# An involution's input turned by VectorE and stored in 128 byte pieces, and a shorter lag for GpSimd while keys are made

## The chip, the cores and the metric

The kernel runs on one core of a Trainium2 chip. The metric is the time of the device in microseconds (us); lower is better. Names used below: PE is TensorE, DVE is VectorE, ACT is ScalarE, POOL is GpSimd, SP is the engine that issues most DMA transfers. Each engine works through its own instructions in order and waits for others through semaphores.

## The reference, cut to what matters

Two layers run one after the other on x, 4 images of 512 channels and 64x64 pixels, all in float32.

```python
# layer 0: attention over the 4096 pixels of each image, CI = 128
q, k, v = wq@x + bq, wk@x + bk, wv@x + bv        # 128 x 4096 each
attn = softmax(q.T @ k, axis=-1)                 # 4096 x 4096
x = wo @ (v @ attn.T) + bo + x
# layer 1: involution with a 7x7 window
o1 = relu(W1@x * s1 + b1)                        # 512 -> 128 channels
w = Ws @ relu(Wr@o1 * sr + br) + bs              # 49 weights per pixel for each of 8 groups of 16 channels
y[c] = sum over 49 taps of w[group(c), tap] * o1[c] shifted by the tap
x = W3@y * s3 + b3 + x
```

## The kernel before, in words

**Attention.** For each image b, `keys_values` goes through eight chunks of 512 pixels (order 2 to 7, then 1, 0), loads x and makes k (matmuls `pk`) and v (`pv`). Then `attention` goes through eight blocks of 512 queries. A block has 32 steps; a step makes one tile of scores (`pss`), ACT takes its exponential into `pt` (five buffers), PE adds `pt` times v into `po`, and DVE adds `pt` into `pacc` (L627), for the softmax's sum. Scores run two steps ahead. A step takes PE 1.72 us when nothing else stands in it.

**What is woven in.** After each step, and several times in each chunk of keys, `chores` advances three generators. `finish_block` ends the block of queries before: it normalizes `on`, runs four matmuls `pwo` (each followed by a DVE add, L513), makes `p1` and `o1`, adds a last bias on ACT (L531), and turns o1 to one pixel per partition: four PE transposes into `pp` (L543), an ACT copy to `o1t` (L546), two transfers into the padded image `pix` in DRAM (L550). Then it makes `pr` and `red`, from which the tap weights come. Its steps are `yield`s; the last image (`late`) uses waits on the planner's clock instead. `involution` works on units of 4 image rows: matmuls `pw` give the tap weights, DVE multiplies them with windows of pixels in `ring` (L339, buffers `prod`, four of them), POOL adds the products to `acc` (L363). `turn_unit` and `close_chunk` turn the sum back (`pa`), run four matmuls `py`, each followed by a DVE add (L417), and store the chunk to `out_dram` (L426).

**The ring.** `pump` loads rows of `pix` into `ring` (L245), 12 rows of windows, as soon as the rows are written and their places are free. It waits on SP for the transfers that wrote them.

**What sets the order.** A planner in Python holds a clock for PE (`pe`) and the times at which DVE, POOL and the DMA will be free by its own costs, and decides at each call whether the next tap product is issued now. The rule that matters here is in `involution`: a product waits while POOL is planned to be more than 7.5 us behind PE. The build then sets each engine's final order, which can move instructions and transfers on a queue by some places; loads of x stand earlier there than the program has them.

**PSUM.** Small matmul results (`pl`, `pwo`, `p1`, `pp`, `pr`, `pa`, `py`, `pq`, and the `spread` that DVE writes) share the tag `mm` with two banks: a result can be written when the one before the last has been read.

Of the kernel before, what the change touches and what calls it, by code (L numbers as in the profile page):

```python
# [8 lines left out]
F32 = mybir.dt.float32  # L9
# [4 lines left out]
B, C, H, W = 4, 512, 64, 64  # L14
N = H * W
P = 128
CT = C // P
CH = 512
NCH = N // CH
RW = CH // W  # L20
# [4 lines left out]
PAD = 3  # L25
# [42 lines left out]
DVE_OP, POOL_OP = 0.7, 1.28  # L68
DVE_TAPS, POOL_TAPS = (0.16, 0.27), (0.19, 0.55)
ROW_US, X_US, PIX_US, LAND_US = 2.2, 3.8, 1.5, 3.0  # L70
HOP_US = 0.8
STEP_US = 1.0
PIECE = 3
TB = 32
WARM = 8
# [5 lines left out]
def fast_path(  # L81
# [20 lines left out]
    nc = tc.nc  # L102

    def pool(name, bufs, **kw):
# [7 lines left out]
    work1 = pool("work1", 1)  # L112
# [3 lines left out]
    ps = pool("ps", 2, space=bass.MemoryType.PSUM)  # L116
# [11 lines left out]
    ident = const.tile([P, P], F32, name="ident")  # L128
# [6 lines left out]
    pix = [  # L135
        scratch.tile([H + 2 * PAD, WP, P], F32, tag=f"pix{i}", name=f"pix{i}") for i in range(2)
    ]
# [9 lines left out]
    pe = 0.0  # L147
    due, seen = 0.0, 0.0
    free = {"dve": 0.0, "pool": 0.0, "dma": 0.0}
    tail = []  # L150
    reds, sums_c = {}, {}
    written = {}
    landing = {}
    low, load = 0, 0

    def until(us):
        while pe < us and not tail:
            yield "wait"

    def pe_us(us):  # L160
        nonlocal pe
        pe += us

    def takes(engine, us):
        free[engine] = max(free[engine], pe) + us
        return free[engine]
# [33 lines left out]
    def w_slice(off, t):  # L200
        return wt[:, off + t * P : off + (t + 1) * P]
# [87 lines left out]
    def involution():  # L289
        nonlocal low, due  # L290
        while True:
            while not units:
                yield "none"
            b, u = units.pop(0)
# [12 lines left out]
            for o, (x, dy, n) in enumerate(ops):  # L307
                if o and dy >= DYS[1][0] > ops[o - 1][1]:
                    low = base + UR
                    pump()  # L310
                    if tail and units:
                        early[units[0]] = weights(*units[0])
                rows = [(base + dy + t * 2) % RING for t in range(NT)]
                while base + dy + n + NT > load:
                    yield "wait"
                landed = max(landing[base + dy + i] for i in range(n + NT))
                while not tail and (
                    pe < max(begin, landed)
                    or free["dve"] > pe + (4.5 if b == B - 1 else 3.5)
                    or free["pool"] > pe + 7.5  # L320
                ):
                    yield "wait"
                free["pool"] = max(free["pool"], takes("dve", DVE_TAPS[0] + DVE_TAPS[1] * n))
                takes("pool", POOL_TAPS[0] + POOL_TAPS[1] * n)
                due -= n
                d0 = dy - DYS[dy >= DYS[1][0]][0]
                first = x == 0 and dy < DYS[1][0]
                prod, p0 = acc, d0
                if not first:
                    prod, p0 = prods.tile(  # L330
                        [P, NT, 4, P], F32, tag="prod", name=f"prod_{b}_{u}_{o}"
                    ), 0
                col = (x * K + dy) * G
                lines = ring[:, rows[0] : rows[0] + n, x, :]
                image = bass.AP(
                    tensor=lines.tensor, offset=lines.offset,
                    ap=[lines.ap[0], [(rows[1] - rows[0]) * K * P, NT], [K * P, n], [1, P]],
                )
                nc.vector.tensor_tensor(  # L339
                    prod[:, :, p0 : p0 + n, :].rearrange("p t d (g c) -> p t d g c", g=G),  # L340
                    image.rearrange("p t d (g c) -> p t d g c", g=G),
                    pw[:, :, col : col + n * G].unsqueeze(3)
                    .broadcast_to([P, NT, n * G, GC])
                    .rearrange("p t (d g) c -> p t d g c", d=n),
                    ALU.mult,
                )
                if first:
                    pass
                elif tail and o % 2 and (accp is not None or n > 1):

                    begin_sum = accp is None
                    if begin_sum:
                        accp = ps1.tile(
                            [P, NT, 2, P], F32, tag=("po", "acc")[u % 2], name=f"accp_{b}_{u}"
                        )
                    for d in range(0, n, 2):
                        k = min(2, n - d)
                        mm(
                            accp[:, :, :k, :], ident, prod[:, :, d : d + k, :],
                            begin_sum and d == 0, o + 2 >= len(ops) and d + 2 >= n,  # L360
                        )
                else:
                    nc.gpsimd.tensor_tensor(  # L363
                        acc[:, :, d0 : d0 + n, :], acc[:, :, d0 : d0 + n, :], prod[:, :, :n, :],
                        ALU.add,
                    )
                yield
# [61 lines left out]
    def keys_values(b):  # L429
        kt = kvpool.tile([P, N], F32, tag="k", name=f"k_{b}")  # L430
        vT = kvpool.tile([P, N // P, P], F32, tag="v", name=f"v_{b}")

        for i, c in enumerate(KEYS):
            for k in KEYS[i + 1 : i + 3]:
                if (b, k) not in xs:
                    load_x(b, k)
            if b < 2 and i == 4:
                for rows in (slice(0, PAD), slice(PAD + H, None)):
                    nc.sync.dma_start(pix[b][rows].rearrange("r w c -> w r c"), zero)
                for cols in (slice(0, PAD), slice(PAD + W, None)):  # L440
                    nc.sync.dma_start(pix[b][PAD : PAD + H, cols, :], zero[:H])
            xt = xs[b, c] if c < KEEP else xs.pop((b, c))
            pk = ps_s.tile([P, CH], F32, tag="s", name=f"pk_{b}_{c}")
            for t in range(CT):
                mm(pk, w_slice(O_WK, t), xt[:, t, :], t == 0, t == CT - 1)
                if t % 2:
                    chores()
            nc.scalar.activation(
                kt[:, c * CH : (c + 1) * CH], pk, AF.Identity, bias=v1(V_BK)
            )  # L450
            pv = ps1.tile([P, 4, P], F32, tag=("po", "acc")[i % 2], name=f"pv_{b}_{c}")
            for j in range(4):
                for t in range(CT):
                    mm(
                        pv[:, j, :], xt[:, t, j * P : (j + 1) * P], w_slice(O_WV, t),
                        t == 0, t == CT - 1,
                    )
                if j % 2:
                    chores()
            nc.scalar.copy(vT[:, 4 * c : 4 * c + 4, :], pv)  # L460
        return kt, vT
# [11 lines left out]
    def finish_block(b, c, off, n, po, sums):  # L473

        late = b == B - 1
        name = f"{b}_{c}_{off}"
# [11 lines left out]
        blocks = work2.tile([P, CH // TB], F32, tag="blocks", name=f"blocks_{name}")  # L488
# [8 lines left out]
        row = (b * N + c * CH + off) // TB  # L497
# [27 lines left out]
        o1 = work1.tile([P, CH], F32, tag="o1", name=f"o1_{name}")[:, :n]  # L525
        nc.scalar.activation(o1, p1, AF.Relu, bias=v1(V_B1), scale=v1(V_S1))

        def last_bias():

            for t in range(CT):  # L530
                nc.scalar.activation(xt[:, t, :], xt[:, t, :], AF.Identity, bias=v1(V_B3 + t))  # L531
                if t % 2:
                    yield

        if late:
            yield from until(pe + HOP_US)
        else:
            yield from last_bias()

        tiles = n // P  # L540
        pp = ps.tile([P, CH // P, P], F32, tag="mm", name=f"pp_{name}")[:, :tiles]
        for t in range(tiles):
            nc.tensor.transpose(pp[:, t, :], o1[:, t * P : (t + 1) * P], ident)  # L543
        pe_us(0.5)
        o1t = work1.tile([P, CH // P, P], F32, tag="o1t", name=f"o1t_{name}")[:, :tiles]
        nc.scalar.copy(o1t, pp)  # L546
        top = c * RW + off // W
        for h in range(2):
            row = PAD + top + h
            nc.sync.dma_start(  # L550
                pix[b % 2][row : row + 2 * tiles - 1 : 2, PAD : PAD + W, :]
                .rearrange("r w c -> w r c"),
                o1t[h * W : (h + 1) * W],
            )
        us = takes("dma", PIX_US) + LAND_US

        pr = ps.tile([P, CH // NT], F32, tag="mm", name=f"pr_{name}")[:, : n // NT]
# [77 lines left out]

    taps = [involution()]
    for b in range(B):
        kv = keys_values(b)
        if b == 0:

            pb = ps.tile([P, CT], F32, tag="mm", name="pb")
            for t in range(CT):
                tc.keep_in_program_order(mm(pb[:, t : t + 1], w_slice(O_WO, t), v1(V_BVC)))
            bo = const.tile([P, CT], F32, name="bo")
            nc.vector.tensor_tensor(bo, pb, vec[:, V_BO : V_BO + CT], ALU.add)
        attention(b, *kv)
# [407 lines left out]
```

## Time and profile before

| | us |
|---|---|
| median of 3 runs | 2645.77 (2645.48 to 2646.93) |
| the profiled execution's own time | 2645.35 |
| its span, first to last instruction | 2643.6 |
| PE busy | 2614.5 |
| DVE busy | 1851.5 |
| POOL busy | 1821.4 |
| ACT busy | 870.0 |

The mean granted clock of TensorE is 0.996. The keys of the four images begin near 5, 620, 1265 and 1910 us; attention of the last image ends near 2560 us, and what follows is the end of the last involution. The 62 transfers of 128 KB into `pix` land 2.5 us after their issue in the median, the loads of x (1 MB) 5.5 us, the stores (1 MB) 4.2 us, and the ring's loads of six rows 15.8 us. In a list of instructions a line gives start, duration, engine, line of the code, operation, output and inputs, shape and count; in square brackets stands the idle time before it and what ended it.

### The profile page before, as it was taken

To read this page: it belongs to the slowest core of one execution; us is meant where nothing else is said; L and a number is where in the kernel's file an instruction comes from. 1 tells how busy PE (TensorE), PEld (TensorE's weight loads), DVE (VectorE), ACT (ScalarE), POOL (GpSimd) and SP (SyncE) were. 2 spreads that over 40 slices of the span, in tenths; PEclk is the share of its full clock that TensorE was granted. 3 is DMA by queue.
4 is the path that set the end of the run, shared out by engine and by line. 5 is a ranking of instruction groups with operands and counts; after the bars stand their busy time and mean duration, and the time that the engine had idled before them with its cause. 6 is when DMAs were issued, how large, how long until landed. Compare 5 with 4: busy or idle time off the path is not lost.

```text
span 2643.6 us, 24069 instructions
## 1 busy us (share of the span) xinstructions
PE 2614.5 (99%) x7478; PEld 1254.9 (47%) x7478; DVE 1851.5 (70%) x2602; ACT 870.0 (33%) x1454; POOL 1821.4 (69%) x1197
## 2 busy tenths in 40 slices
PE   9999999999999999999999999999999999999998
PEld 7444444445544444444554444444464444444574
DVE  0437788776575778778566677878847667787887
ACT  1333333332333333333223333333323333333330
POOL 0007788788761788888784377878888467777875
PEclk9999999999999999999999999999999999999999
DMA  6032323325614233332450423333353423222343
GB/s 233 0 74 60 92 66 77 77 57 140 157 35 105 60 92 92 92 82 65 121 143 13 106 60 92 92 92 92 92 142 107 97 60 85 69 62 61 75 90 100
DMA packets 104730, 231.70 MB, mean 88 GB/s; under 512 B 5576, under 2 KB 24464, under 8 KB 104464
## 3 DMA queue, kind: packets, MB, share of 16 engines
q1 hardware_dynamic: 104160, 229.70, 35.2%
q8 instruction: 61, 1.00, 0.2%
q14 instruction: 77, 0.63, 0.1%
q10 hardware_dynamic: 432, 0.36, 0.0%
HBM read 187.28 MB, written 42.77 MB: 87 GB/s over the span
## 4 chain that ended last, share of the span: by engine, by line
PE 91%; POOL 4%; DMA 2%; DVE 2%; issue 1%; ACT 0%; SPq 0%; POOLq 0%; DVEq 0%; ACTq 0%
PE pss L208 32%; PE po L208 32%; POOL acc L363 4%; PE pq L208 4%; PE p L208 4%; PE py L208 4%; PE pwo L208 4%; PE pv L208 3%; PE pk L208 3%; DMA ring<-pix 2%; PE pw L208 2%; DVE prod L339 1%; PE pr L208 1%; PE pp L543 1%; PE accp L208 0%
## 5 line engine op out<-in xcount | busy, mean ns | idle before, releaser
L363 POOL TENSOR_TENSOR acc<-acc,prod 128x768 f32<-128x768 f32 (+3 forms) x1063 | 1699.6, 1619 | 797.5 <-DVE prod L339 694.7
L208 PE MATMUL pss<-q,k 128*128 128x512 f32 (+1 forms) x2112 | 1055.2, 584 | 2.3 <-ACT q L469 2.3
L208 PE MATMUL po<-pt,v 128*128 128x512 f32 (+1 forms) x2112 | 1047.0, 580 | 0.0
L596 ACT ACTIVATE pt<-pss 128x512 f32<-128x512 f32 x1024 | 611.2, 597 | 1219.0 <-PE pss L208 1198.7
L339 DVE TENSOR_TENSOR prod<-ring,pw 128x512 f32<-128x512 f32 (+3 forms) x1092 | 899.9, 849 | 147.6 <-POOL acc L363 93.4
L627 DVE TENSOR_TENSOR pacc<-pacc,pt 128x512 f32<-128x512 f32 x958 | 665.3, 695 | 415.6 <-ACT pt L596 405.9
L208 PEld LDWEIGHTS po<-pt,v 128*128 128x128 f32 x2112 | 398.6, 190 | 477.5 <-issue 458.7
L208 PEld LDWEIGHTS pss<-q,k 128*128 128x128 f32 x2112 | 389.3, 190 | 455.0 <-issue 436.3
L208 PE MATMUL py<-accT,wt 128*128 128x512 f32 (+1 forms) x264 | 133.0, 587 | 13.8 <-DVE x L513 12.7
L417 DVE SCALAR_TENSOR_TENSOR x<-py,vec,x 128x512 f32<-128x512 f32 (+1 forms) x132 | 96.4, 730 | 53.6 <-PE py L208 51.6
L208 PEld LDWEIGHTS pv<-wt,x 128*128 128x128 f32 x1024 | 123.3, 198 | 14.8 <-issue 14.8
L208 PE MATMUL pwo<-on,wt 128*128 128x512 f32 (+1 forms) x264 | 129.2, 582 | 0.0
L374 POOL TENSOR_TENSOR acc<-acc 128x512 f32<-128x512 f32 x120 | 119.7, 997 | 9.4
L208 PE MATMUL pv<-wt,x 128*128 128x128 f32 x1024 | 126.0, 282 | 0.0
L339 DVE TENSOR_TENSOR acc<-ring,pw 128x1024 f32<-128x1024 f32 (+1 forms) x84 | 79.4, 964 | 62.4 <-PE pw L208 60.6
L531 ACT ACTIVATE x<-x,vec 128x512 f32<-128x512 f32 (+1 forms) x132 | 92.9, 706 | 81.5 <-PE p L208 76.3
L208 PE MATMUL p<-x,wt 128*128 128x512 f32 (+1 forms) x264 | 119.2, 579 | 0.0
L208 PE MATMUL pk<-x,wt 128*128 128x512 f32 x256 | 117.3, 597 | 0.0
L208 PE MATMUL pq<-x,wt 128*128 128x512 f32 (+1 forms) x264 | 115.6, 580 | 0.0
L513 DVE SCALAR_TENSOR_TENSOR x<-pwo,bo,x 128x512 f32<-128x512 f32 (+1 forms) x132 | 96.4, 733 | 23.6 <-PE pwo L208 20.4
L208 PEld LDWEIGHTS py<-accT,wt 128*128 128x128 f32 x264 | 49.5, 191 | 72.9 <-issue 43.3
L208 PEld LDWEIGHTS pq<-x,wt 128*128 128x128 f32 x264 | 49.7, 190 | 58.8 <-issue 52.7
(57 smaller groups left out, 747.7 us busy)
## 6 DMA issues: line engine op xcount, KB each, us to landing
x<-x_dram SPq DMA_DIRECT2D x55, 1024.0 KB, 5.5
ring<-pix SPq DMA_DIRECT2D x74, 448.0 KB, 10.4
ring<-pix SPq DMA_DIRECT2D x24, 1344.0 KB, 15.8
out_dram<-x SPq DMA_DIRECT2D x31, 1024.0 KB, 4.2
ring<-pix SPq DMA_DIRECT2D x24, 896.0 KB, 13.6
ring<-pix SPq DMA_DIRECT2D x30, 672.0 KB, 10.9
ring<-pix SPq DMA_DIRECT2D x6, 2240.0 KB, 21.0
pix<-o1t SPq DMA_DIRECT2D x62, 128.0 KB, 2.5
```

The lines of the kernel that those rows point to most:

```text
L208: return nc.tensor.matmul(o, lhsT=lhsT, rhs=rhs, start=start, stop=stop)
L339: nc.vector.tensor_tensor(prod[:, :, p0 : p0 + n, :].rearrange("p t d (g c) -> p t d g c", g=G), image.rearrange("p t d (g c) -> p t d g c ...
L363: nc.gpsimd.tensor_tensor(acc[:, :, d0 : d0 + n, :], acc[:, :, d0 : d0 + n, :], prod[:, :, :n, :], ALU.add,)
L374: nc.gpsimd.tensor_tensor(acc[:, :, :n, :], acc[:, :, :n, :], acc[:, :, n : 2 * n, :], ALU.add)
L417: nc.vector.scalar_tensor_tensor(xt[:, t, :], py, v1(V_S3 + t), xt[:, t, :], ALU.mult, ALU.add)
L513: nc.vector.scalar_tensor_tensor(xt[:, t, :], pw, bo[:, t : t + 1], xt[:, t, :], ALU.add, ALU.add)
L531: nc.scalar.activation(xt[:, t, :], xt[:, t, :], AF.Identity, bias=v1(V_B3 + t))
L543: nc.tensor.transpose(pp[:, t, :], o1[:, t * P : (t + 1) * P], ident)
L596: nc.scalar.activation(pt, pss, AF.Exp)
L627: nc.vector.tensor_tensor(paccs[k], paccs[k], pt, ALU.add)
```

## The change

First, the lag. The limit of 7.5 us becomes a variable: 4.0 us while `keys_values(b)` runs, 7.5 us in attention.

Second, for images 0 to 2 the turn of o1 changes. DVE transposes the 128x512 tile in blocks of 32x32 into `o1t`, directly after o1. Partition 32i+a then holds, for each run of 32 pixels, pixel a of the run and the 32 channels of group i. PE's four transposes and ACT's copy are gone. Eight transfers, one for each group of channels and half of the image's width, put it in place, each in 256 pieces of 32 floats (128 bytes); before, there were two transfers of 256 pieces of 512 bytes. They are issued three yields after the last bias, and `pr`, `red` and the entry of the units follow them. The last image keeps PE's transposes.

```diff
+POOL_LAG = 4.0, 7.5
@@ involution
-                    or free["pool"] > pe + 7.5
+                    or free["pool"] > pe + lag
@@ finish_block
+        o1t = work1.tile([P, CH // P, P], F32, tag="o1t", name=f"o1t_{name}")[:, :tiles]
         if late:
             yield from until(pe + HOP_US)
+            (transposes pp, copy to o1t and two transfers, as before)
         else:
+            blocks = o1t.rearrange("p t c -> p (t c)")
+            takes("dve", DVE_OP)
+            nc.vector.transpose(
+                blocks.rearrange("p (k q) -> p k q", q=TB), o1.rearrange("p (k q) -> p k q", q=TB)
+            )
             yield from last_bias()
-        (transposes pp, copy to o1t and two transfers, for every image)
+            for _ in range(3):
+                yield
+            for i in range(P // TB):
+                channels = slice(i * TB, (i + 1) * TB)
+                for h in range(W // TB):
+                    columns = slice(PAD + h * TB, PAD + (h + 1) * TB)
+                    nc.sync.dma_start(
+                        pix[b % 2][PAD + top : PAD + top + RW, columns, channels]
+                        .rearrange("r a c -> a r c"),
+                        blocks[channels].rearrange("p (r h c) -> p r h c", r=RW, c=TB)[:, :, h, :],
+                    )
@@ the loop over images
+        lag = POOL_LAG[0]
         kv = keys_values(b)
+        lag = POOL_LAG[1]
```

More of the change, by code (lines that the diff above doesn't have):

```diff
@@ L153, in fast_path @@
     landing = {}
+    lag = 0.0
     low, load = 0, 0
@@ L533, in last_bias @@
                     yield
+        tiles = n // P
+        top = c * RW + off // W
+        o1t = work1.tile([P, CH // P, P], F32, tag="o1t", name=f"o1t_{name}")[:, :tiles]
         if late:
             yield from until(pe + HOP_US)
-        else:
-            yield from last_bias()
[L540 to L554, printed above, removed]
+            pp = ps.tile([P, CH // P, P], F32, tag="mm", name=f"pp_{name}")[:, :tiles]
@@ new lines, in finish_block @@
+            for t in range(tiles):
+                nc.tensor.transpose(pp[:, t, :], o1[:, t * P : (t + 1) * P], ident)
+            pe_us(0.5)
+            nc.scalar.copy(o1t, pp)
+            for h in range(2):
+                row = PAD + top + h
+                nc.sync.dma_start(
+                    pix[b % 2][row : row + 2 * tiles - 1 : 2, PAD : PAD + W, :]
+                    .rearrange("r w c -> w r c"),
+                    o1t[h * W : (h + 1) * W],
+                )
+        else:
+            blocks = o1t.rearrange("p t c -> p (t c)")
[3 more added lines that the diff above has]
+            )
+            yield from last_bias()
+            for _ in range(3):
[4 more added lines that the diff above has]
+                    columns = slice(PAD + h * TB, PAD + (h + 1) * TB)
+                    nc.sync.dma_start(
+                        pix[b % 2][PAD + top : PAD + top + RW, columns, channels]
+                        .rearrange("r a c -> a r c"),
+                        blocks[channels].rearrange("p (r h c) -> p r h c", r=RW, c=TB)[:, :, h, :],
+                    )
```

## The prediction

> **What bounds the kernel now.** I read the busy times first, then what TensorE waits for, then the timeline around its longest wait.
>
> ```profile
> PE 2614.5 (99%) x7478; PEld 1254.9 (47%) x7478; DVE 1851.5 (70%) x2602; ACT 870.0 (33%) x1454; POOL 1821.4 (69%) x1197
> ```
>
> TensorE (PE) is busy for 2614.5 of 2643.6 us. Only two things shorten the program: fewer PE instructions, or fewer of the 29.1 us in which PE stands idle. The waits of PE say where those are:
>
> ```profile
> PE py L208 <- DVE x L513: 12.7, 3, 4.5
> PE accp L208 <- DVE prod L339: 2.4, 1, 2.4
> PE pss L208 <- ACT q L469: 2.3, 3, 0.8
> ```
>
> The first line is three waits, at 650, 1295 and 1940 us: once in each keys stage that has an involution beside it. About 12 us more lie after 2540 us, in the end game. The timeline of PE, then of VectorE (DVE), at the first wait (start, duration, line, names):
>
> ```profile
> 646.97 3.60 PE L208 MATMUL pk<-x,wt 128*128 128x512 f32 x8
> 654.52 1.30 PE L208 MATMUL py<-accT,wt 128*128 128x512 f32 x2 [3.95 <-DVE x L513]
> 655.61 5.24 PE L208 MATMUL pv<-wt,x 128*128 128x128 f32 x32
> 660.69 1.88 PE L208 MATMUL p<-x,wt 128*128 128x512 f32 x4
> ...
> 689.35 3.60 PE L208 MATMUL pk<-x,wt 128*128 128x512 f32 x8
> 692.78 3.73 PE L208 MATMUL pv<-wt,x 128*128 128x128 f32 x32
> 696.36 3.60 PE L208 MATMUL pq<-x,wt 128*128 128x512 f32 x8
> ```
>
> ```profile
> 650.97 0.95 DVE L339 TENSOR_TENSOR prod<-ring,pw 128x768 f32<-128x768 f32 x1 [1.47 <-POOL acc L363]
> 652.85 0.95 DVE L339 TENSOR_TENSOR prod<-ring,pw 128x768 f32<-128x768 f32 x1 [0.93 <-POOL acc L363]
> 653.72 0.75 DVE L513 SCALAR_TENSOR_TENSOR x<-pwo,bo,x 128x512 f32<-128x512 f32 x1
> ```
>
> py needs a `mm` bank of PSUM that the L513 add of the last pwo must read first. That add stands in DVE's order behind five tap products, and each of these waits for GpSimd (POOL) to give back one of four prod buffers. PE falls idle 3.95 us and then runs slowly: pv x32 takes 5.08 us (655.61 to 660.69), against 3.58 at 692.78. From the start of pk to the start of p the undisturbed cost is 3.43 (pk, 689.35 to 692.78) + 0.86 (one py) + 3.58 (pv) = 7.87 us; the trace has 13.72 here, 14.78 (1291.36 to 1306.14) and 13.97 (1936.57 to 1950.54). **The three waits cost 5.9 + 6.9 + 6.1 = 18.9 us**, not 12.7.
>
> **What the Trainium skill says.** "TensorE: Matmul & The Clock Gate", Part 1 (the HAM clock gate): an idle window of about 3.4 us drops the array to half clock until it has been busy again. The trace agrees: granted clock 0.65 from 656 to 660 us, 1.00 from 660. "VectorE: DVE Perf Modes", The three transpose paths: VectorE turns 32x32 blocks only, so a run of contiguous channels after it is 32 floats; no SBUF to SBUF turn is in this trace, and the nearest row is the 718 ns stream transpose of L502. "DMA: Bandwidth & Descriptors", Specifications: below 512 B a transfer is a read-modify-write; no such transfer of the program can be picked out in this trace. Same page, Queues, rings and completion order: each DMA engine takes descriptors in ring order, so what is issued behind the pieces starts behind them.
>
> **The change part by part.**
>
> *1. 96 transposes leave PE* (4 for each of the 24 blocks of batches 0 to 2; the last batch keeps its path).
>
> ```profile
> 597.26 0.60 PE L543 MATMUL pp<-ident,o 128*128 128x128 f32 x4
> 597.79 0.65 PE L208 MATMUL pr<-o,wt 128*64 128x256 f32 x4
> ```
>
> From the first pp to the next instruction 0.53 us pass, the same at 672.11, 1317.57 and 1961.97. PE does not idle there, so 24 x 0.53 = **12.7 us** come off.
>
> *2. The lag of 4.0 in the keys stage* sends tap products later relative to PE. In the built order of the changed kernel rls, spread and on now precede the seven last products of unit 11; the first three L513 adds follow these, still ahead of unit 12; the fourth L513 add stands behind four products of unit 12 instead of twelve. I walked it on PE's durations, with the old kernel's clock up to 589.5 us. The keys stage starts at about 619.6, pl is there at 623.2, unit 11's products run from about 625 to 632 (POOL takes 1.9 us each), the three adds follow their pwo at 633 to 640, pw of unit 12 comes at 640, the fourth add at 646 with py wanting its bank at 655. The tightest spot is the last py (665.3): its bank is freed by an L417 add standing behind a product that waits for POOL's eighth 768-or-wider sum of unit 12 (643.2 + 6 x 2.43 + 2 x 1.9 = 661.6), done at 663.3. Slack 2.0 us; the chain before it has another 1.8 (POOL ends unit 11 at 641.4). So all 18.9 us should go; if POOL is 4 us later than this, part returns. Bounds 0 to 18.9; I take **18.9**, since the wait needs a shift of the order, which was made, and the slack is positive at each bank.
>
> *3. 24 stream transposes join DVE*, 24 x 0.72 (L502) = 17.3 us. In attention (330 to 590 us) DVE is busy 208.6 of 260 us, so each 72 us block has some 14 us free for 0.72; with that cover gone it would cost up to 17.3. Behind each stand taps, a pacc add and L417 adds. PE tolerates DVE about three steps behind (five pt buffers, scores two steps ahead), 3 x 1.72 = 5.2 us. ScalarE loses 24 copies of 0.585 us; at 33% busy, worth nothing.
>
> *4. The pix transfers.* Two DMAs of 256 pieces of 512 B become eight of 256 pieces of 128 B: SP issues for 8 x 0.61 = 4.9 us instead of 1.2. The first pix pair of the trace, alone, kept the engines at shares 0.16, 0.78, 0.84 and 0.40 in four half microseconds: 17.4 us of engine time for 512 pieces, 34 ns each. For 2048 pieces I take the same 34 ns: 4.4 us over 16 engines, under the issue time. Bounds: 8.5 ns (bytes alone, 1.1 us) and 68 ns (read and write back, 8.7 us). The ring load waits for all eight. In SP's new order six stand ahead of the out_dram store and two behind it, then the x load, which waits 4.2 us for that store (its landing), then the ring. SP in the old kernel around it:
>
> ```profile
> 596.30 0.39 SPq L426 DMA_DIRECT2D out_dram<-x  x1
> 598.51 1.27 SPq L550 DMA_DIRECT2D pix<-o1t  x2
> 600.54 0.37 SPq L171 DMA_DIRECT2D x<-x_dram  x1
> 601.71 10.66 SPq L245 DMA_DIRECT2D ring<-pix  x4
> ```
>
> The store's trigger (last L417 add) moves to about 598.3, so the ring goes out at about 603, 1.3 us later than 601.7; with 68 ns some 6 us later. The first product that reads it moves later too, by about three steps in attention (the planner counts from the delayed program point) and to 625 here, where the old load landed at 619.9. Hidden at 34 ns, mostly at 68.
>
> *5. In the keys stage six pieces stand on SP ahead of the load of x chunk 0*: they wait for the turn at about 665, so the load goes out near 669 and lands 5.5 us later (median of x loads), 675; held up behind the pieces, 680. PE wants it for the last pk at 682. Nothing, with little to spare.
>
> *6. The end.* The pw and pa of units move three to six steps later, up to the second block of the next batch; from the fourth block of batch 3 on the order of PE and POOL is that of the old kernel, and PE is 240 of 240 us busy from 2300 to 2540. The time gained before passes to the end unchanged.
>
> *Allowance* for small new waits of PE at 24 changed blocks: 0 to 6 us, I take 2.
>
> Sum against the profiled span: 2643.6 - 12.7 - 18.9 + 2 = 2614.0. That execution took 2645.35 us, 1.75 around the span; the median of the runs is 2645.77, so 2.2 above the span: **2616.2 us**.
>
> **Rivals.** *A, a wait in place of the removed one* (20%): POOL, a bank or x chunk 0 comes late in the keys stage. For: slacks of 2 to 6 us. Against: each is positive. All three back: 2616.2 + 18.9 = 2635; half of it 2626. *B, VectorE carries the turns onto the path in attention* (8%): 0.3 to 0.72 us per block, 7 to 17 us: 2623 to 2633. Against: its 14 us free per block. *C, slower* (7%): the 128 B pieces are so dear that the ring is late in every block. For: no piece this small is measured; in attention the old kernel already waits for the ring 0.2 to 0.7 us at 464, 1108 and 2157. Each block then loses what exceeds about 4 us of gained slack and 5.2 us of tolerance. The gain of 31.6 us is gone at 1.3 us per block, with the ring some 10.5 us late, that is pix landing some 18 us after its start instead of 3.7: 18 us / 128 pieces per engine = about 140 ns per piece, four times the 512 B piece. At 180 ns it adds 5 us more per block: about 2645.8 + 24 x 5 = 2766. *D, the lag does nothing to the stalls* is A at its full 2635.
>
> **How the numbers follow.** The forecast (both gains, 0 to 6 us given back) has 62%, range 2613 to 2621; A 20%, B 8%, C 7%, a gain above the forecast 3%. Range 2611 to 2633: it leaves out C, the worst third of A and the far gain, under 2 in 10. Within 0.2% (5.3 us, about what a measurement can tell from no change) of 2645.8 means 2640.5 to 2651: only A with B, or a mild C: 4%. Slower 7%, faster 89%.
>
> **What would show it.** Right: no pp group of 128 but 32, PE busy down by about 12.7 plus the slow-clock share; no PE wait of 4 us on L513 in a keys stage, and pv x32 near 3.6 throughout; a stream transpose o1t<-o x24 of about 0.7 us; pix landing within about 10 us; end game of the same length. Wrong: PE waits for L417, pr or pk in the keys stage (A), pss waiting for ACT behind late pacc adds (B), DVE products waiting many us for ring in attention (C).

## The result, and the profile after

The changed kernel takes 2623.33 us (2623.28 to 2624.13, 4 runs), the kernel before 2645.95 us beside it: a ratio of 0.9916, 95% interval 0.9901 to 0.9931. It is 22.6 us faster, where 29.6 were forecast. The time lies in the range given; it lies 7.1 us above the forecast, and most of this document is about those 7 us and about what had really earned the other 22.

The busy times of the page after:

```profile
PE 2599.3 (99%) x7382; PEld 1242.0 (47%) x7382; DVE 1865.5 (71%) x2626; ACT 857.2 (33%) x1430; POOL 1821.0 (69%) x1197
```

PE executes 96 instructions fewer and is busy 15.2 us less. Over a span of 2622.3 us it idles 23.0 us instead of 29.1, so 15.2 + 6.1 = 21.3 us, which is the difference of the spans. The longest waits of PE after (what it waited for, total, times, longest) show a new first line:

```profile
PE py L210 <- DVE x L419: 6.7, 3, 2.4
PE accp L210 <- DVE prod L341: 2.4, 1, 2.4
```

The old kernel's 12.7 us on the L513 add are gone. In their place, once in each of the same three keys stages, a `py` waits for the add of another `py` (L417 before, L419 now). PE's timeline at two of the three:

```profile
656.76 1.88 PE L210 MATMUL pk<-x,wt 128*128 128x512 f32 x4
661.06 2.03 PE L210 MATMUL py<-accT,wt 128*128 128x512 f32 x2 [2.42 <-DVE x L419]
662.89 4.54 PE L210 MATMUL pv<-wt,x 128*128 128x128 f32 x32
667.26 1.02 PE L210 MATMUL py<-accT,wt 128*128 128x512 f32 x2
...
1299.68 1.12 PE L210 MATMUL py<-accT,wt 128*128 128x512 f32 x2 [2.13 <-DVE x L419]
1300.64 3.73 PE L210 MATMUL pv<-wt,x 128*128 128x128 f32 x32
```

From the start of the `pk` x4 to the start of the second `py` behind it the undisturbed cost is 1.72 (pk) + 0.86 (py) + 3.57 (pv) = 6.15 us. The trace has 10.50 here, 8.54 at 1295.67 and 10.20 at 1932.62: losses of 4.35 + 2.39 + 4.05 = 10.8 us, where the old kernel lost 18.9. DVE's timeline says why:

```profile
657.51 0.95 DVE L341 TENSOR_TENSOR prod<-ring,pw 128x768 f32<-128x768 f32 x1 [0.94 <-POOL acc L365]
659.39 0.96 DVE L341 TENSOR_TENSOR prod<-ring,pw 128x768 f32<-128x768 f32 x1 [0.93 <-POOL acc L365]
660.26 0.74 DVE L419 SCALAR_TENSOR_TENSOR x<-py,vec,x 128x512 f32<-128x512 f32 x1
```

The add that frees the bank stands behind products that go at POOL's pace, and ends at 661.0; PE had wanted the bank since 658.6. It is the old stall with another add in it.

The new work is cheap. The turn, among the groups of instructions (busy time and mean ns behind the first bar, idle time before it behind the second), and the pieces, among the DMA issues (KB of each, median us to landing):

```profile
L559 DVE STREAM_TRANSPOSE o1t<-o 128x512 f32<-128x512 f32 x24 | 17.0, 707 | 17.2 <-ACT o L528 17.2
```

```profile
pix<-o1t SPq DMA_DIRECT2D x192, 32.0 KB, 1.7
```

### The profile page after: what moved, and what is told of

It is laid out like the page before. It is cut to its first block, busy times and chain, and to the rows that moved or that the text cites. A ratio compares the mean times of both kernels' runs of the same rounds, so it can differ in the third digit from the quotient of the medians.

```text
span 2622.3 us, 24098 instructions
## 1 busy us (share of the span) xinstructions
PE 2599.3 (99%) x7382; PEld 1242.0 (47%) x7382; DVE 1865.5 (71%) x2626; ACT 857.2 (33%) x1430; POOL 1821.0 (69%) x1197
## 4 chain that ended last, share of the span: by engine, by line
PE 94%; POOL 3%; DVE 2%; DMA 0%; issue 0%; ACT 0%; POOLq 0%; DVEq 0%; ACTq 0%
PE pss L210 34%; PE po L210 33%; PE pq L210 4%; PE pwo L210 4%; PE p L210 4%; PE py L210 4%; PE pv L210 4%; PE pk L210 3%; POOL acc L365 3%; PE pw L210 2%; DVE prod L341 1%; PE pr L210 1%; PE pa L393 0%; PE accp L210 0%; DVE x L419 0%
## 5 line engine op out<-in xcount | busy, mean ns | idle before, releaser
L210 PEld LDWEIGHTS pv<-wt,x 128*128 128x128 f32 x1024 | 121.7, 195 | 15.8 <-issue 15.6
L515 DVE SCALAR_TENSOR_TENSOR x<-pwo,bo,x 128x512 f32<-128x512 f32 (+1 forms) x132 | 96.3, 734 | 45.5 <-PE pwo L210 44.0
L419 DVE SCALAR_TENSOR_TENSOR x<-py,vec,x 128x512 f32<-128x512 f32 (+1 forms) x132 | 95.9, 726 | 29.8 <-PE py L210 28.1
```

Source lines behind the costliest of these rows:

```text
L210: return nc.tensor.matmul(o, lhsT=lhsT, rhs=rhs, start=start, stop=stop)
L419: nc.vector.scalar_tensor_tensor(xt[:, t, :], py, v1(V_S3 + t), xt[:, t, :], ALU.mult, ALU.add)
L515: nc.vector.scalar_tensor_tensor(xt[:, t, :], pw, bo[:, t : t + 1], xt[:, t, :], ALU.add, ALU.add)
```

## The experiments

Each kernel ran beside the kernel before on the same chip (medians of that kernel 2644.8 to 2645.3 us). The change has three separable parts: the turn with its pieces, the three yields ahead of the transfers ("late issue" from here on), and the lag. PE's idle time is its span less its busy time.

| kernel | turn by | issue | lag in keys | us | ratio to before | PE busy | PE idle |
|---|---|---|---|---|---|---|---|
| before | PE | at once | 7.5 | 2645.95 | 1 | 2614.5 | 29.1 |
| after | DVE | late | 4.0 | 2623.33 | 0.9916 | 2599.3 | 23.0 |
| e1_lag_only | PE | at once | 4.0 | 2631.88 | 0.9949 | 2608.5 | 22.5 |
| e2_turn_only | DVE | late | 7.5 | 2623.56 | 0.9918 | 2599.2 | 23.1 |
| e5_late_only | PE | late | 7.5 | 2632.62 | 0.9953 | 2609.3 | 21.4 |
| e6_turn_at_once | DVE | at once | 7.5 | 2654.99 | 1.0039 | 2611.8 | 41.2 |
| e12_lag_4_at_once | DVE | at once | 4.0 | 2645.80 | 1.0003 | 2607.5 | 35.9 |
| e3_py_apart | DVE | late | 4.0 | 2614.31 | 0.9884 | 2596.3 | 16.2 |
| e10_turn_apart_lag_7 | DVE | late | 7.5 | 2613.46 | 0.9882 | 2594.8 | 16.2 |
| e4_lag_2 | DVE | late | 2.0 | 2614.26 | 0.9885 | 2594.6 | 17.5 |
| e11_lag_2_apart | DVE | late | 2.0 | 2611.60 | 0.9874 | 2595.0 | 14.6 |
| e9_all_but_turn | PE | late | 4.0 | 2661.47 | 1.0062 | 2620.4 | 39.5 |
| e7_turn_twice | DVE, twice | late | 4.0 | 2624.32 | 0.9921 | 2600.7 | 22.6 |
| e8_pieces_of_64 | DVE | late | 4.0 | 2625.72 | 0.9925 | 2600.7 | 23.3 |

The ratios' intervals reach about 0.0016 to either side (e12: 0.0009). In e3, e9, e10 and e11 the four `py` stand further apart.

### The lag alone, and everything but the lag

My theory after the result was that the lag had taken away 8 of the stalls' 18.9 us (Theory 1); the rival, that the lag brings nothing and the other parts of the change moved the order (Theory 2).

```diff
 e1_lag_only: before, with POOL_LAG = 4.0, 7.5
 e2_turn_only: after, with
-POOL_LAG = 4.0, 7.5
+POOL_LAG = 7.5, 7.5
```

> The kernel before with the lag of 4.0 us in the keys stages alone; PE's transposes and the two 512 byte transfers stay. Theory 1 (the lag is what shortened the keys stalls, about 8 us over three stages): about 2638 us. Theory 2 (the lag matters only together with the later turn, since each alone merely moves which bank PE waits for): between 2639 and 2646 us, with a PE wait of some 3 us for an L419-like add of the second py in each keys stage, in place of the wait for the fourth pwo add.

> The changed kernel with 7.5 us of lag everywhere: only the turn and its transfers. Theory 1: the 12.7 us of the transposes alone, 2633 us, and keys stalls of 4 us as before. Theory 2: the later turn already moves the normalization ahead of unit 11's last products, so the keys stalls fall to about 2.3 us as in the changed kernel, and the time is 2622 to 2626 us: then the lag edit is worth next to nothing beside the turn.

Both theories were half wrong. The lag alone is worth 12.9 us (2644.8 to 2631.9), more than Theory 1 had and against Theory 2. When it is taken out of the changed kernel, the time rises by 0.2 us, which is nothing, as Theory 2 had it. The waits of PE in the first:

```profile
PE py L210 <- DVE x L419: 5.1, 3, 1.7
...
PE py L210 <- DVE x L515: 1.7, 3, 0.8
```

and in the second:

```profile
PE py L210 <- DVE x L419: 7.8, 3, 2.8
```

Either edit takes most of the wait on the add of `pwo` (L513 before, L515 here) away, and either has a wait on the add of `py` (L419) in its place. Two edits that lift the same stall don't add up. It remained open which part of the second kernel lifts it: the missing transposes, or the late issue.

### The late issue alone, and the turn without it

```diff
 e5_late_only: before, with
         nc.scalar.copy(o1t, pp)
+        if not late:
+            for _ in range(3):
+                yield
 e6_turn_at_once: e2_turn_only, with
-            for _ in range(3):
-                yield
```

> One part of the change alone: the transposes stay on TensorE and the lag is 7.5 everywhere, but the pix transfers of the first three batches are issued three steps later, as in the changed kernel. Theory late issue (the three steps put off the planned landing of pix, so the planner begins the involution's next unit later, and the L515 adds come ahead of its products): about 8.5 us of the stalls go, as with the turn alone, 2636 to 2639, with py waiting for the L419 add 2 to 3 us. Rival transposes (the stalls shortened because TensorE lost its transposes): nothing here, 2645 to 2647, with the old waits of about 4 us on L515.

> The turn by VectorE with its pieces, lag 7.5 everywhere, but the pieces are issued at once, without the three steps. Theory late issue: only the transposes' 12.7 us go and the stalls stay, 2631 to 2635, with py waiting about 4 us for an L515 add. Rival transposes: as with the turn alone, 2623 to 2625.

The late issue alone is worth 12.7 us (2645.3 to 2632.6), against the transposes as the reason. It is 3 us below the expected range: its waits on L419 are 1.8 us at the longest, not 2 to 3, and the granted clock is 0.999. The instruction order shows the way: in the old kernel the `pw` of the involution's next unit goes to PE ahead of the first `pwo`, and with the late issue behind the second one, at the same lag. Before:

```profile
630.92 0.93 PE L208 MATMUL pw<-wt,red 33*128 33x392 f32 x4
631.77 2.05 PE L208 MATMUL pv<-wt,x 128*128 128x128 f32 x16
633.66 1.02 PE L208 MATMUL pwo<-on,wt 128*128 128x512 f32 x2
```

and with the late issue:

```profile
637.30 1.02 PE L210 MATMUL pwo<-on,wt 128*128 128x512 f32 x2
638.25 0.93 PE L210 MATMUL pw<-wt,red 33*128 33x392 f32 x4
```

The planner takes the pieces to land later, begins the unit later, and the L515 adds come ahead of its products. (`pr` and `red`, which stand behind the three yields in the program, come later too; no run parts the two.)

The second run went outside both expectations: the turn without the late issue is slower than the old kernel, by 9.7 us. Its waits of PE:

```profile
PE pk L210 <- DMA x<-x_dram: 16.1, 3, 6.3
PE py L210 <- DVE x L515: 11.1, 3, 3.7
```

The second line is the old stall, as expected. The first is new. PE's timeline in this kernel, in the first of the three stages:

```profile
682.08 3.73 PE L210 MATMUL pv<-wt,x 128*128 128x128 f32 x32
692.09 5.31 PE L210 MATMUL pk<-x,wt 128*128 128x512 f32 x8 [6.28 <-DMA x<-x_dram]
```

And SP's transfers ahead of it there:

```profile
665.19 3.78 SPq L567 DMA_DIRECT2D pix<-o1t  x8
669.07 0.40 SPq L428 DMA_DIRECT2D out_dram<-x  x1
670.28 3.27 SPq L247 DMA_DIRECT2D ring<-pix  x4
673.59 0.60 SPq L173 DMA_DIRECT2D x<-x_dram  x1
```

against SP in the changed kernel:

```profile
662.88 2.79 SPq L569 DMA_DIRECT2D pix<-o1t  x6
667.46 0.39 SPq L173 DMA_DIRECT2D x<-x_dram  x1
667.89 1.00 SPq L569 DMA_DIRECT2D pix<-o1t  x2
...
674.00 12.81 SPq L247 DMA_DIRECT2D ring<-pix  x6
```

The x load is that of chunk 0, which the last `pk` of the stage reads. In the changed kernel it stands among the pieces and ahead of the ring loads; without the three yields four ring loads come first, and x lands 18.4 us after its issue. At the same place in the next keys stage of the changed kernel (1304.4 us) it lands 5.8 us after. Each of the three stages then idles 4.3 to 6.3 us more and runs on at a lower clock: the `pk` x8 behind the wait takes 5.31, 6.39 and 6.42 us, instead of 3.60 without a wait, and the granted clock is 0.58 from 692 to 696 us.

### The same with a lag of 4.0

```diff
 e12_lag_4_at_once: after, with
-            for _ in range(3):
-                yield
```

> The changed kernel without the three steps: lag 4.0, the turn, the pieces issued at once. The x load of chunk 0 stands behind four ring loads, as in e6_turn_at_once. If that order is what made e6_turn_at_once slow, PE again waits some 5 us for x in each of three keys stages, with a slow clock after it, and the lag takes off only the L515 waits: 2638 to 2646. If the late issue works through the start of unit 12 alone, the lag does the same here: 2622 to 2626.

2645.8 us: no different from the kernel before, at the slow edge of the first expectation. PE's first wait is the same as in e6_turn_at_once:

```profile
PE pk L210 <- DMA x<-x_dram: 16.0, 3, 6.5
```

The shorter lag took 9.2 us off, from the waits on L515 (11.1 to 1.1 us, with 5.1 on L419 in their place), and left the x load where it was:

```profile
PE py L210 <- DVE x L419: 5.1, 3, 1.7
...
PE py L210 <- DVE x L515: 1.1, 3, 0.6
```

The start of the unit alone is therefore not the whole effect of the late issue: beside the turn, the three yields are worth 22.5 us at a lag of 4.0 and 31.4 at 7.5, and the x load's place on SP is the larger part of it by the traces (16 us of PE's waits, and the clock after them). No run moved the x load by itself.

### The bank that is left

The L419 wait was put to the test in two ways: by moving the `py` apart, so that the one that needs the bank comes later on PE, and by a still shorter lag, so that fewer products stand ahead of the add.

```diff
 e3_py_apart: after, in close_chunk
-            for _ in range(2):
+            for _ in range(4 if lag == POOL_LAG[0] else 2):
                 yield
 e4_lag_2: after, with
-POOL_LAG = 4.0, 7.5
+POOL_LAG = 2.0, 7.5
```

> The changed kernel with four instead of two yields after each py while keys are made: the third py then stands some 7 us later on PE, behind the chunk's pv, the next pk and pr. If what is left of the keys stalls (6.7 us idle, about 10.8 us with the slow clock after it) is the wait of the third py for the bank that the second py's add must read behind products paced by GpSimd, that wait is gone and the time is 2611 to 2615 us. If GpSimd's backlog itself holds PE, the wait moves to another instruction and the time stays near 2623 us.

> The changed kernel with a lag of 2.0 us in the keys stages. If a shorter lag always means a shorter stall: no PE wait left, 2612 to 2616 us. If the stall is set by where the second py's add stands in VectorE's order: unit 12 starts some 5 us later, that add stands behind the unit's last product, and the third py waits 2 to 4 us for it: 2622 to 2630 us.

Each brings some 9 us. In the first the waits on L419 are gone from the list, and PE goes through the place without a break:

```profile
655.45 1.88 PE L210 MATMUL pk<-x,wt 128*128 128x512 f32 x4
657.17 1.02 PE L210 MATMUL py<-accT,wt 128*128 128x512 f32 x2
658.03 3.73 PE L210 MATMUL pv<-wt,x 128*128 128x128 f32 x32
```

In the second, where a wait of 2 to 4 us had been thought possible, `pr` waits 0.9 us at most for an L419 add:

```profile
PE pr L210 <- DVE x L419: 2.1, 3, 0.9
```

Up to the last image's `pl`, where the end game begins (2544.6 us in the changed kernel), the two profiles are 11.3 and 10.5 us ahead, beside the 10.8 worked out from the timeline above; behind it they are 1.5 and 0.3 us longer.

```diff
 e10_turn_apart_lag_7: e3_py_apart, with
-POOL_LAG = 4.0, 7.5
+POOL_LAG = 7.501, 7.5
 e11_lag_2_apart: both mends, e3_py_apart with
+POOL_LAG = 2.0, 7.5
```

(7.501 only keeps the condition in close_chunk able to tell the stages apart.)

> As e3_py_apart, but with the lag of before (7.5) in the keys stage too, so the turn, the late issue and the py set apart. If the lag edit is worth nothing once the late issue has moved unit 12 and the py stand apart: 2613 to 2616. If the shorter lag is still needed for the banks: 2618 to 2624, with PE waiting for an L515 or L419 add.

> The changed kernel with a lag of 2.0 in the keys stage and the py set apart: both mends at once. PE's floor is 2594.6 busy (e4_lag_2) and 16.2 idle (e3_py_apart), a span of 2610.8: 2612 to 2614. If the later units of the involution are missed afterwards (in attention, or in the end game): 2617 or more.

Without the lag edit the spread `py` give 2613.5 us: with the late issue and the `py` apart, the lag is worth nothing. Both mends together give 2611.6 us, the lowest median here and a little below the range expected, 1.3% below the kernel before (0.9874, interval 0.9857 to 0.9890). Its PE is busy:

```profile
PE 2595.0 (99%) x7382; PEld 1238.7 (47%) x7382; DVE 1866.3 (72%) x2626; ACT 856.8 (33%) x1430; POOL 1821.6 (70%) x1197
```

of 2609.6 us; what is left of idle time, 14.6 us, is mostly the end game's (11.9 us after the last image's `pl` at 2532.2 us).

### The price of the transposes by itself

```diff
 e9_all_but_turn: e5_late_only, with
+POOL_LAG = 4.0, 7.5
 and in close_chunk
-            for _ in range(2):
+            for _ in range(4 if lag == POOL_LAG[0] else 2):
```

> The changed kernel with the py instructions set apart (as in e3_py_apart), but with the transposes back on TensorE and the pix pieces of 512 bytes: what is left of the difference from e3_py_apart is the turn alone, with no stall on either side. Step 1's price of 24 x 0.53 = 12.7 us above e3_py_apart's 2614.3: 2626 to 2628, with PE idle some 16 us. If the turn also saves or costs something elsewhere (attention, pieces), 2623 or less, or 2630 or more.

The total, 2661.5 us, is the slowest of all. It lies in the open range of 2630 or more, but that was meant for a turn that saves something elsewhere, and the reason is another. Its waits of PE begin with

```profile
PE pw L210 <- DVE prod L341: 25.8, 3, 8.6
```

and the place is the first step of attention:

```profile
690.65 3.60 PE L210 MATMUL pq<-x,wt 128*128 128x512 f32 x8
702.87 1.64 PE L210 MATMUL pw<-wt,red 33*128 33x392 f32 x2 [8.62 <-DVE prod L341]
```

The weights of the next unit (`pw`) go to PE right behind `pq`; their bank is read by the unit before, whose products leave DVE at POOL's pace until 702.7:

```profile
699.71 1.11 DVE L341 TENSOR_TENSOR prod<-ring,pw 128x512 f32<-128x512 f32 x2 [0.80 <-POOL acc L365]
701.62 1.11 DVE L341 TENSOR_TENSOR prod<-ring,pw 128x512 f32<-128x512 f32 x2 [0.80 <-POOL acc L365]
```

In e3_py_apart that `pw` stands at 708.2, after nine steps of attention, and waits for nothing. So the run doesn't give the whole price. It gives it up to that place. `pq` starts at 690.65, where e3_py_apart starts it at 686.39, and up to there PE has idled 1.05 us in either run, all of it near the start of the program. Eight blocks' transposes lie before: 4.26 / 8 = 0.53 us each, as step 1 had it.

### The turn and the pieces

```diff
 e7_turn_twice: after, with
+            nc.vector.transpose(
+                blocks.rearrange("p (k q) -> p k q", q=TB), o1.rearrange("p (k q) -> p k q", q=TB)
+            )
 e8_pieces_of_64: after; every transfer in two, of 16 channels each
+                    for s in range(2):
+                        channels = slice(i * TB + s * HP, i * TB + (s + 1) * HP)
```

> The changed kernel with each of the 24 stream transposes made twice into the same tile: 17 us more work of VectorE, everything else in the same order. Hidden, as step 3 has it: 2623 to 2625. On the path, as rival B has it: 7 to 17 us more, 2630 to 2640.

> The changed kernel with each piece cut in two: 16 transfers per block of 256 pieces of 64 bytes, 4096 pieces instead of 2048. Step 4's price of 34 ns per piece and 0.45 us of issue: pix lands some 4 us later, the ring load goes out some 4 us later, mostly hidden, 2623 to 2627. Rival C's price of 140 ns or more per piece: 256 pieces per engine take 36 us, each block loses several us, 2660 or more.

Doubling the turn adds 15.8 us to DVE's busy time (1881.3) and 1.0 us to the run, with overlapping intervals (0.9904 to 0.9937 and 0.9901 to 0.9931): the turn is hidden. Twice as many pieces of half the size add 2.4 us, intervals overlapping again (0.9908 to 0.9942). SP now issues for 8.62 us at the first block, where it took 3.79, but a transfer still lands in 1.7 us in the median:

```profile
pix<-o1t SPq DMA_DIRECT2D x384, 16.0 KB, 1.7
```

## Why the prediction was right, and where it was wrong

*The sum.* Its terms were 12.7 for the transposes, 18.9 for the stalls and 2 given back. With 18.9 - 10.8 = 8.1 for the stalls the span comes to 2643.6 - 12.7 - 8.1 = 2622.8; measured are 2622.3. The end game, which had no term, was 2.0 us shorter (step 6), so some 1.5 us were given back elsewhere, inside the allowance of 0 to 6. The median of the runs lies 1.0 us above the profiled span, not 2.2. Errors: +10.8 for the stalls, -0.5 for the allowance, -2.0 for the end game, -1.2 for the median, +7.1 us in all. The three small ones, all below zero, made up for a third of the large one; that was luck.

*Step 1* held: 0.53 us per block, measured without a stall between e9_all_but_turn and e3_py_apart. Two groups of kernels agree more loosely: at a clock of 0.999 PE is busy 2608.5 and 2609.3 us with transposes (e1, e5) and 2594.6 to 2595.0 without (e4, e10, e11).

*Step 2 failed*, twice. First in size: "The tightest spot is the last py (665.3)" is one `py` too late. The traces of the change show the third `py` waiting for the add of the second, and the last one free. The walk had given PE's small results their banks in PE's order as I read it, and so gave the bank to the wrong `py`. The add itself was the right one, behind the product that waits for POOL's eighth sum. The walk had it done at 663.3 and the last `py` at 665.3; the third `py` stands one `py` and one `pv` earlier (0.86 + 3.57 us), at 660.9, which is 2.4 us too early, and 2.42 us were measured (wanted at 658.6, freed at 661.0). "All 18.9 us should go" became 8.1. So what happened is rival A, and its sign, PE waiting for L417 (L419 now) in the keys stage, stands in the trace, as do `pv` x32 of 4.54 and 5.36 us where 3.6 throughout was the sign of being right. The rival was priced from 2626; the measured time lies between it and the forecast, and inside a range that was drawn wide enough for most of A.

Second in cause: "the wait needs a shift of the order, which was made" was put down to the lag. e2_turn_only makes the same shift with the old lag. The three yields, which steps 4 and 5 counted only as a delay of transfers, move the unit's start as the lag does. Nothing of the 22.6 us needs the lag edit. The walk was made on the built order, which has the effect of the yields in it; so it could find the shift and still name the wrong cause.

*Step 3* held: 24 turns of 707 ns, hidden even when doubled, so rival B is out. ScalarE is busy 12.8 us less. DVE waits 17.2 us for the ReLU ahead of the turn, which the step didn't have; among PE's waits for DVE the add of `py` is the only new line.

*Step 4* held in its verdict and was too dear in its price. The ring went out at 602.8, forecast 603. A piece of 128 bytes takes 13.7 ns of engine time, not 34 (below), a tenth of the 140 ns at which rival C was to eat the gain.

*Step 5* held for the kernel as it is: the x load went out at 667.5, not 669, and PE didn't wait for it. But its "nothing, with little to spare" was the most fragile part of the change, and not for the pieces' sake: without the late issue the ring loads go ahead of x, and the whole gain and more is lost (e6, e12). The trace of before had shown the x load one place ahead of the ring's (674.72 and 675.85 us in the first keys stage); the prediction didn't ask what held it there. What in the planner decides this place wasn't followed up.

*Step 6* held in the order: from the last image's `pl` (2563.9 us before, 2544.6 after) PE runs the same instructions to the end. It takes 79.7 us for them before and 77.7 after. In the profiles of the fourteen kernels here the stretch takes 77.1 to 79.7 us, with PE busy for 65.5 to 65.6 us in eight and for 66.6 to 67.2 in six. Before, four `accp` behind a wait for POOL took 3.19 us, after 1.88. With one profile of a kernel it stays open whether the 2.0 us belong to the change.

## What to carry to other kernels

Two edits that lift one stall are worth it once: before adding their gains, ask of each whether the other already removes the wait. Where an order is planned, a delay put in for one thing (here a transfer) moves others with it, and its largest effect may be which transfer stands ahead on a shared queue. When a wait on a rotating bank is removed, walk the banks again in the built order, one allocation at a time: the next wait is likely the same stall, one tile further on.

## What the runs showed of the hardware

*Small pieces.* The first block's 2048 pieces of 128 bytes are alone on the queue at 165 to 169.5 us. The windows of half a microsecond there (the last two columns are the share of the 16 DMA engines and GB/s) are like these two, but for the last (0.58 and 93):

```profile
166.00:166.50 0.50, 0.50 (x3) 0.26 (x2) 0.15 (x1) 0.32 (x1) 0.00 (x0) 1.00 0.43 66
166.50:167.00 0.50, 0.50 (x3) 0.26 (x2) 0.50 (x1) 0.00 (x0) 0.00 (x0) 1.00 0.41 66
```

The shares of the eight windows sum to 3.50; 3.50 x 0.5 us x 16 engines / 2048 = 13.7 ns per piece, where 512 bytes took 34. For the same bytes that is more engine time, 28.0 us against 17.4. With shares near 0.4 the engines are not the limit; it is SP's issue, eight transfers in 3.79 us or 0.47 us each. The Trainium skill ("DMA: Bandwidth & Descriptors", Specifications) says that a transfer below 512 bytes is a read-modify-write; if it was one here, it made a piece no dearer than a larger one.

*The clock after short idle times.* Idle times are those of the profile, which models the ends of matmuls. The three waits of 2.42, 2.13 and 2.16 us in the changed kernel cost 4.35, 2.39 and 4.05 us: after the first and the third PE ran slowly (pv x32 in 4.54 and 5.36 us), after the second it didn't (3.73). In e2_turn_only waits of 2.60 and 2.78 us were followed by a slow stretch, one of 2.42 wasn't, and the waits of at most 1.8 us in e1 and e5 left the mean clock at 0.999. The skill's page on the clock gate ("TensorE: Matmul & The Clock Gate", Part 1) has an idle window of about 3.4 us; here 2.2 us could be enough, and 2.4 us could pass. What these waits cost is therefore read from the trace, not from their length. The granted clock (third column from the right) behind the three of the changed kernel:

```profile
663.00:665.00 2.00, 2.00 (x13) 2.00 (x12) 0.75 (x1) 0.00 (x0) 1.92 (x2) 0.61 0.31 49
1302.00:1304.00 2.00, 2.00 (x21) 2.00 (x20) 0.10 (x1) 0.00 (x0) 1.92 (x2) 1.00 0.37 58
1939.00:1941.00 2.00, 2.00 (x12) 2.00 (x11) 0.08 (x1) 0.00 (x0) 1.92 (x2) 0.50 0.37 59
```
